# A first layer norm two slots sooner, transposed in 32 by 32 blocks on VectorE and through DRAM

## The chip, the cores and the metric

The kernel runs on one core of a Trainium2 chip. The metric is device time in microseconds of one execution: 1315.79 us as the median of three runs (1315.71 to 1316.1). TensorE does the matrix products, VectorE, ScalarE and GpSimd the elementwise work, SyncE (SP) issues nearly all DMAs. Each of these works through its own instructions in the order in which the kernel writes them.

## The reference

One decoder layer in float32 over `x` of 16 batches, 512 tokens, 256 features. Cut to what matters (B=16, T=512, D=256, 16 heads of 16 dimensions, hidden width 1024):

```python
q = query @ wq + query @ Aq @ Bq * 4;  k = query @ wk;  v = query @ wv + query @ Av @ Bv * 4
q, k = rope(split(q)), rope(split(k))
scores = where(causal, -1e9, einsum('bhqd,bhkd->bhqk', q, k) / 4)
x = layernorm(x + merge(softmax(scores) @ split(v)) @ wo)          # the first norm
h = gelu(butterfly(x @ W_exp + b_exp, up_weights) + up_bias)       # the expansion
y = butterfly(h, down_weights) @ W_con + b_con + down_bias         # the contraction
out = layernorm(x + y)                                             # the second norm
```

## The kernel before

The butterflies are folded into the weights during the first batches, so the feed-forward part of a batch is two dense products: `wup` (256 x 1024) for the expansion and `wdn` (1024 x 256) for the contraction. A batch's residual lies in `zs[b]`, with 128 tokens on the partitions, four token tiles of 256 features.

Everything is laid out on a time table of slots, written by hand. A batch has 20 slots (`per`), so batch b starts at slot s = 20 b, and slot s+41 of batch b is also slot s+21 of batch b+1, s+1 of batch b+2 and s+61 of batch b-1. Four batches are in flight. In every slot the loop at the end of `decoder_layer` issues in this order: score matmuls of two kinds, interleaved in pairs (`weights`, transposed scores that are to be exponentiated, and, 15 slots ahead of them, `largest`, scores whose maxima are wanted); then for each of them what reads it (ScalarE's exponential and GpSimd's causal mask for `weights`, VectorE's masked reductions at L426 for `largest`); then `weigh`, the products of finished exponentials with v; then the functions entered in `others[slot]`, in the order in which they were entered (a lower batch first); then those of `holes[slot]`. The score matmuls of a slot write two PSUM tiles, `pb` and `pa`, each with a single buffer: the next slot's matmuls can only start on them when the readers are through. In most slots `pb` is read by the exponential and `pa` by the reductions; in the last of each five slots both are read by both. All other matmuls take one of three PSUM banks (`bank`).

The feed-forward of batch b follows its attention in these steps, by slot:

- s+40, s+41: `project_out` (the product with wo, L589) and `add_attention` (L601: VectorE adds it to `zs[b]` and takes statistics, one tile at a time); the last tile's `add_attention` in s+42.
- s+42: `spread` (L616: VectorE adds epsilon, GpSimd raises to the power -0.5). s+43, first in the slot: `offset` (L628, VectorE). s+44: `centre` (L635: four ScalarE activations that normalize `zs[b]`).
- s+45: `turn_x1` (L647): eight TensorE transposes of 128 x 128, two VectorE copies into `x1T`, and a GpSimd addition of the bias to `zs[b]` (s+46 for batch 14).
- s+46 to s+49: `hidden` (L664), the expansion in eight chunks of 128 units, two a slot; VectorE copies chunks 0 and 4 out of PSUM, ScalarE the others. s+50: `gelus`. For batch 14 the chunks come in s+47 and later, for batch 15 all at the end.
- s+51 to s+58: `contract` (L691) for tiles 0 to 2, half of the hidden units at a time, and tile 3 in s+63 and s+64, then the second norm (`spread` s+65, `offset` s+67, `centre` and `store` s+68).

In the same slots lie the following of other batches: `project_v` of batch b+2 (its v projections, at s+39 for tile 1, s+42 for tile 2, s+52 for tile 3); the rotary products of batch b+2's q and k on GpSimd (`turn`); `place_largest` of batch b+1 in s+41 (L440: a VectorE transpose of maxima, a DMA to DRAM and two DMAs that put them as a row into q); and `gather` and `invert` of batch b+1 in s+45 and s+46 (a chain of small DMAs for the softmax sums). The softmax of batch b+1 goes on without pause.

Of the kernel before, what the change touches and what calls it, by code (L numbers as in the profile page):

```python
# [11 lines left out]
F32 = mybir.dt.float32  # L12
BF16 = mybir.dt.bfloat16
AF = mybir.ActivationFunctionType
ALU = mybir.AluOpType
PSUM = bass.MemoryType.PSUM

P = 128
NH = 16
DH = 16  # L20
HG = 32
NG = P // HG
# [11 lines left out]
def decoder_layer(  # L34
# [18 lines left out]
    nc = tc.nc  # L53
    B, T, D = x.shape
    NT = T // P
    NC = D // P
    DHID = wcon.shape[0]
    NHC = DHID // P
# [5 lines left out]
    ring2 = ctx.enter_context(tc.tile_pool(name="ring2", bufs=2))  # L64
# [3 lines left out]
    dram = ctx.enter_context(tc.tile_pool(name="dram", bufs=4, space=bass.MemoryType.DRAM))  # L68
# [5 lines left out]
    def bank(name, shape):  # L74
        return ps_w.tile(shape, F32, tag="w", name=name)

    def columns(out, w, moving, start, stop):

        for g in range(NG):
            part = slice(HG * g, HG * (g + 1))  # L80
            nc.tensor.matmul(out[part, :], w[:, part], moving, start=start, stop=stop)  # L81
# [10 lines left out]
    xTs, zs = {}, {}  # L92
# [23 lines left out]
    wdn = const.tile([P, NHC, D], F32, name="wdn")  # L116
    bias2 = const.tile([P, 2, D], F32, name="bias2")
# [337 lines left out]
    state = {}  # L455
# [151 lines left out]
    def stats_of(which, b, t):  # L607
        if t == 0:
            state["stats", which, b] = small.tile(
                [P, NT, 2], F32, tag=f"stats{which}", name=f"stats{which}_{b}"  # L610
            )
        bn = small.tile([P, nc.vector.BN_STATS_DIM], F32, tag="bn", name=f"bn{which}_{b}_{t}")
        nc.vector.bn_stats(bn, zs[b][:, t, :])
        nc.vector.bn_aggr(state["stats", which, b][:, t, :], bn)
# [13 lines left out]
    def offset(which, b, t0=0, t1=NT):  # L628
        stats, norm = state["stats", which, b], state["norm", which, b]
        ts = slice(t0, t1)  # L630
        nc.vector.scalar_tensor_tensor(  # L631
            norm[:, 2, ts], stats[:, ts, 0], -1.0, norm[:, 1, ts], ALU.mult, ALU.mult
        )
# [10 lines left out]
            )  # L644


    def turn_x1(b, c):  # L647
        if c == 0:
            state["x1T", b] = ring2.tile([P, NC, T], F32, tag="x1T", name=f"x1T_{b}", bufs=1)
        pt = bank(f"pt1_{b}_{c}", [P, NT, P])  # L650
        for t in range(NT):
            nc.tensor.transpose(pt[:, t, :], zs[b][:, t, c * P : (c + 1) * P], ident)  # L652
        nc.vector.tensor_copy(
            state["x1T", b][:, c, :], pt.rearrange("p t q -> p (t q)")
        )
        if c == NC - 1:
            nc.gpsimd.tensor_tensor(
                zs[b],
                zs[b],
                bias2[:, 0:1, :].to_broadcast([P, NT, D]),  # L660
                ALU.add,
            )
# [21 lines left out]
    def gelus(b, count=NHC):  # L684
        h = state["h", b]
        for hc in range(count):
            nc.scalar.activation(  # L687
                h[:, hc, :], h[:, hc, :], AF.Gelu, bias=hbias[:, hc : hc + 1]
            )

    def contract(b, t, half):  # L691
        if half == 0:
            state["py"] = bank(f"py_{b}_{t}", [P, D])
        py = state["py"]
        for hc in range(half * NHC // 2, (half + 1) * NHC // 2):
            columns(
                py,
                state["h", b][:, hc, t * P : (t + 1) * P],
                wdn[:, hc, :],
                hc == 0,  # L700
                hc == NHC - 1,
            )
        if half == 1:
            nc.vector.tensor_add(zs[b][:, t, :], py, zs[b][:, t, :])  # L704
            stats_of(2, b, t)

    def store(b):
        nc.sync.dma_start(out[b].rearrange("(t p) d -> p t d", p=P), zs[b])
# [14 lines left out]
    end = B * per + behind  # L723
    last = end + 8
    head = 2
    others = {s: [] for s in range(-head, last)}
    holes = {}
    chains = [(c, side) for c in range(NC) for side in range(2)]

    def add(s, f, *args):  # L730
        others[s].append(lambda: f(*args))

    def start_projection(b, side, c):
        state["pr", b, side, c] = project(b, side, c)
# [13 lines left out]
    for b in range(B):  # L748
        s = b * per
        if b > 0:  # L750

            at = {1: (-16, -11, -13, -9), B - 1: (-3, 2, 10, 10)}.get(b, (-3, -1, 2, 12))
            for t in range(NT):
                add(s + at[t], project_v, b, t)
        if b + 1 < B:

            add(s - head * (b == 0), load_xT, b + 1)
            at = {0: (2, 5, 7, 10), 1: (3, 6, 8, 11)}.get(b, (10, 10, 10, 10))
            for i, (c, side) in enumerate(chains):
                holes.setdefault(s + at[i], []).append(  # L760
                    lambda b=b, side=side, c=c: start_projection(b + 1, side, c)
                )
                turning = s + max(at[0] + 1 + 3 * i, at[i] + 1)
                for step in range(3):
                    add(turning + step, turn, b + 1, side, c, step)
                for step in range(1 + side):
                    add(turning + (6 if i == 3 else 4) + step, part, b + 1, side, c, step)
        add(s + 9, load_x, b)
        add(s + 11, place_largest, b, 0)
        add(s + 21, place_largest, b, 1)  # L770
        for c in range(NC if b + 1 < B else 1):
            if c + 1 < NC:
                add(s + 25 + (b + 1 == B), gather, b, c)
            add(s + (26, 36)[c] + (b + 1 == B), invert, b, c)
            for t in range(NT):
                add(s + ((29, 29, 30, 30), (39, 39, 40, 40))[c][t], scale, b, c, t)
        if b + 1 < B:
            for t in range(NT):
                add(s + (40, 40, 41, 41)[t], project_out, b, t)
                add(s + (40, 40, 41, 42)[t], add_attention, b, t)  # L780
            add(s + 42, spread, 1, b)
            others[s + 43].insert(0, lambda b=b: offset(1, b))
            add(s + 44, centre, 1, b)
            for c in range(NC):
                add(s + 45 + (b + 2 == B), turn_x1, b, c)
        if b + 2 < B:

            late = 2 * (b + 3 == B)
            for hc in range(NHC - late):
                add(s + 46 + hc // 2, hidden, b, hc)  # L790
            holes.setdefault(s + 50, []).insert(0, lambda b=b, late=late: gelus(b, NHC - late))
            for hc in range(NHC - late, NHC):
                holes[s + 50].append(lambda b=b, hc=hc: hidden(b, hc, True))
            for t in range(NT):
                for half in range(2):
                    at = (11, 13, 14, 15, 16, 18, 23, 24)[2 * t + half]
                    if b + 3 == B and t == NT - 1:
                        at = (23, 25)[half]
                    add(s + 40 + at, contract, b, t, half)
            add(s + 65, spread, 2, b)  # L800
            add(s + 67, offset, 2, b)
            add(s + 68, centre, 2, b)
            add(s + 68, store, b)
# [3 lines left out]
    y, z = B - 2, B - 1  # L807
# [4 lines left out]
    for hc, at in ((3, 10), (4, 10), (5, 10), (6, 11), (7, 11)):  # L812
        add(edge + at, hidden, y, hc, True)

    add(end - 3, contract, y, 0, 0)
    add(end - 1, contract, y, 0, 1)
    add(end + 2, contract, y, 1, 0)
    add(end + 2, contract, y, 1, 1)
    for t in range(NT):
        add(end + 2, normalize, z, NC - 1, t)  # L820
    add(end + 2, contract, y, 2, 0)
    for t in range(NT + 1):
        if t < NT:
            add(end + 3, project_out, z, t)
# [2 lines left out]
        if t > 0:  # L827
            add(end + 3, offset, 1, z, t - 1, t)
            add(end + 3, centre, 1, z, t - 1, t)
    add(end + 3, contract, y, 2, 1)  # L830
    add(end + 3, contract, y, 3, 0)
    for c in range(NC):
        add(end + 5, turn_x1, z, c)
    add(end + 5, contract, y, 3, 1)
    for hc in range(NHC):
        add(end + 5, hidden, z, hc, True)
    add(end + 5, spread, 2, y)
# [2 lines left out]
    add(end + 6, store, y)  # L840
    for t in range(NT):
        for half in range(2):
            add(end + 7, contract, z, t, half)
        add(end + 7, finish_tile, z, t)


    first, second = fold_tasks()
# [180 lines left out]
```

## Time and profile before

| what | value |
|---|---|
| median of 3 runs | 1315.79 us |
| profiled execution | 1318.97 us, its span 1317.0 us |
| VectorE, ScalarE, GpSimd busy | 59%, 53%, 43% of the span |
| DMA, mean share of 16 engines | about 18%, 74 MB |
| transposes `pt` (L652) | 128 of 280 ns |
| copies `x1T` (L653) | 32 of 678 ns |
| centre (L638) | 128 of 589 ns |
| mean granted TensorE clock | 0.989 |

The profile is of one execution. A matmul in float32 is listed twice, since the array makes two passes; a transpose is listed once. In a timeline, a line gives start and length in us, engine, source line, operation, output <- inputs, shape and count, and in brackets how long the engine was idle before it and what ended that. The matmuls of a group overlap, so the distance between the starts of two groups is the time that a group cost TensorE. In the table of stretches each engine's busy time stands in the order PE, PEld, DVE, ACT, POOL, then the granted clock, the DMA share and GB/s.

### The profile page before, as it was taken

The numbers are of one execution on the slowest core, as the hardware profiler recorded it, in microseconds if no ns is written. First come the engines' busy times: TensorE is split into PE (matmuls) and PEld (weight loads), VectorE is DVE, ScalarE is ACT, GpSimd is POOL, SyncE is SP. The second block draws the span as 40 slices with busy tenths as digits, with TensorE's granted clock in tenths as the row PEclk, the third lists the DMA queues.
The fourth block names the chain that finished last, engine by engine and source line by source line (L and its number), as shares of the span: only waits on it lengthen the run. The fifth ranks groups of instructions, "written<-read, shape, count | busy, mean of one in ns | idle before, by whom it ended". The sixth has DMA issues, their size and how long they took to land.

```text
span 1317.0 us, 38318 instructions
## 1 busy us (share of the span) xinstructions
PE 1280.6 (97%) x15896; PEld 575.2 (44%) x15896; DVE 780.5 (59%) x2760; ACT 702.9 (53%) x1047; POOL 565.1 (43%) x905
## 2 busy tenths in 40 slices
PE   8888999999999999999999999999999999999998
PEld 3343435444353544435354443535444353444443
DVE  5776746657465665747566574756657474665431
ACT  2574455555646555564655546465555646455643
POOL 4525325445362544536254453625445362532430
PEclk9889999999999999999999999999999999999999
DMA  5411111111212111121211112121211212111101
GB/s 169 132 32 59 40 49 46 56 56 41 82 41 65 47 56 56 41 83 41 69 42 57 56 41 83 41 67 45 56 56 40 83 41 70 41 40 32 43 20 34
DMA packets 64062, 74.07 MB, mean 56 GB/s; under 512 B 23120, under 2 KB 42576, under 8 KB 63888
## 3 DMA queue, kind: packets, MB, share of 16 engines
q1 hardware_dynamic: 60000, 66.07, 16.0%
q10 hardware_dynamic: 3888, 5.55, 1.4%
q8 instruction: 125, 2.05, 0.7%
q14 instruction: 49, 0.40, 0.1%
HBM read 40.17 MB, written 18.06 MB: 44 GB/s over the span
## 4 chain that ended last, share of the span: by engine, by line
PE 92%; DVE 3%; ACT 2%; DMA 1%; issue 1%; POOL 0%; SPq 0%; POOLq 0%; DVEq 0%; ACTq 0%
PE pb L474 21%; PE py L81 17%; PE ph L81 16%; PE po L516 12%; PE pqk L81 8%; PE pa L417 4%; PE pwo L81 4%; PE pvv L81 4%; DVE junk L426 1%; PE pd L81 1%; PE pt L652 1%; PE pa L474 1%; PE pb L417 1%; ACT pT L488 1%; ACT h L687 0%
## 5 line engine op out<-in xcount | busy, mean ns | idle before, releaser
L426 DVE CUSTOM_DVE_ANT_0 junk<-pa,causal 128x384 bf16<-128x384 f32 (+2 forms) x878 | 438.6, 500 | 339.0 <-PE pa L417 271.6
L488 ACT ACTIVATE pT<-pb 128x1024 f32<-128x1024 f32 (+1 forms) x314 | 294.2, 937 | 354.8 <-PE pa L417 183.8
L492 POOL TENSOR_SCALAR_AFFINE_SELECT pT<-pT 128x256 f32<-128x256 f32 x512 | 202.3, 407 | 651.4 <-ACT pT L488 650.4
L474 PE MATMUL pb<-qz,kz 17*128 17x512 f32 (+2 forms) x1756 | 330.9, 475 | 17.6 <-ACT pT L488 11.7
L417 PE MATMUL pa<-kz,qz 32*128 32x384 f32 (+3 forms) x1756 | 330.6, 476 | 3.4 <-DVE mx L426 3.4
L81 PE MATMUL py<-wdn,h 128*32 128x256 f32 x4096 | 244.3, 381 | 0.0
L81 PE MATMUL ph<-x1T,yb 128*32 128x512 f32 x2048 | 231.6, 594 | 0.2 <-ACT h L678 0.2
L474 PEld LDWEIGHTS pb<-qz,kz 17*128 17x128 f32 (+1 forms) x1756 | 142.4, 184 | 196.4 <-issue 92.3
L516 PE MATMUL po<-pT,vaug 128*32 128x512 f32 (+3 forms) x2048 | 180.9, 447 | 1.8 <-POOL pT L492 1.8
L81 PEld LDWEIGHTS py<-wdn,h 128*32 128x32 f32 x4096 | 125.3, 110 | 99.2 <-issue 12.7
L417 PEld LDWEIGHTS pa<-kz,qz 32*128 32x128 f32 (+1 forms) x1756 | 143.2, 185 | 14.6 <-DVE mx L426 11.6
L81 PEld LDWEIGHTS ph<-x1T,yb 128*32 128x32 f32 x2048 | 63.2, 110 | 139.8 <-issue 107.6
L81 PE MATMUL pqk<-xT,wqk 128*32 128x512 f32 x1024 | 117.6, 608 | 0.0
L682 ACT COPY h<-ph 128x512 f32<-128x512 f32 x84 | 49.2, 585 | 117.3 <-PE ph L81 117.2
L516 PEld LDWEIGHTS po<-pT,vaug 128*32 128x32 f32 x2048 | 47.9, 109 | 105.3 <-issue 59.1
L426 DVE DVE_READ_ACCUMULATOR2_ANT mx<- 128x1 f32 x1024 | 84.6, 83 | 0.0
L638 ACT ACTIVATE z<-z,norm 128x256 f32<-128x256 f32 x128 | 66.7, 589 | 23.2 <-DVE norm L631 23.2
L365 POOL TENSOR_TENSOR swap<-swap,rope_sb 128x512 f32<-128x512 f32 x62 | 78.8, 1270 | 0.0
L426 DVE CUSTOM_DVE_ANT_0 junk<-pb,causal 128x256 bf16<-128x256 f32 (+3 forms) x146 | 63.6, 436 | 16.4 <-PE pb L417 2.5
L687 ACT ACTIVATE h<-h,hbias 128x512 f32<-128x512 f32 x113 | 70.8, 709 | 0.2
L704 DVE TENSOR_TENSOR z<-py,z 128x256 f32<-128x256 f32 x64 | 27.2, 425 | 72.9 <-PE py L81 70.6
L81 PE MATMUL pvv<-wv_sb,xT 128*32 128x256 f32 x1024 | 66.5, 379 | 0.0
(91 smaller groups left out, 1192.1 us busy)
## 6 DMA issues: line engine op xcount, KB each, us to landing
xT<-in_xT SPq DMA_DIRECT2D x16, 512.0 KB
swap<-qz SPq DMA_DIRECT2D x64, 128.0 KB
swap<-kz SPq DMA_DIRECT2D x64, 128.0 KB
z<-in_x SPq DMA_DIRECT2D x16, 512.0 KB
wide<-recips SPq DMA_DIRECT2D x31, 256.0 KB
spread<-wide SPq DMA_DIRECT2D x31, 256.0 KB
out_y<-z SPq DMA_DIRECT2D x15, 512.0 KB
x<-x SPq DMA_DIRECT2D x32, 128.0 KB
```

Source lines behind the costliest of these rows:

```text
L81: nc.tensor.matmul(out[part, :], w[:, part], moving, start=start, stop=stop)
L365: engine.tensor_tensor(swap, swap, rope_sb[:, 1, :], ALU.mult)
L417: lambda i=i, rows=rows, at=at, n=n, t=t, ps=ps: nc.tensor.matmul(ps[:, i, at : at + n], q[rows, par, t * P : n], k_[rows, par, 0:n], star ...
L426: lambda i=i, at=at, n=n, t=t, g=g, ps=ps: nc.vector.tensor_tensor_reduce(out=junk[:, 0:n], in0=ps[:, i, at : at + n], in1=causal[:, T - n ...
L474: lambda i=i, rows=rows, at=at, n=n, k=block, ps=ps: nc.tensor.matmul(ps[:, i, at : at + n], kt[rows, par, k * P : (k + 1) * P], qt[rows, ...
L488: nc.scalar.activation(pT[:, heads, 0:n], ps[:, :, at : at + n], AF.Exp)
L492: nc.gpsimd.affine_select(out=diag, in_=diag, pattern=[[0, 2], [1, P]], compare_op=ALU.is_ge, fill=0.0, base=0, channel_multiplier=-1,)
L516: nc.tensor.matmul(po[HG * g : HG * (g + 1), k * P : T], vaugs[b % 2][:, k, NG * c + g, first : first + HG], pT[:, g, at : at + n], start= ...
L638: nc.scalar.activation(zs[b][:, t, :], zs[b][:, t, :], AF.Identity, bias=norm[:, 2, t : t + 1], scale=norm[:, 1, t : t + 1],)
L682: nc.scalar.copy(h, ph)
L687: nc.scalar.activation(h[:, hc, :], h[:, hc, :], AF.Gelu, bias=hbias[:, hc : hc + 1])
L704: nc.vector.tensor_add(zs[b][:, t, :], py, zs[b][:, t, :])
```

## The change

The first norm's last `add_attention` and `spread` move to s+41, `offset` and `centre` to s+42. `turn_x1` is replaced, in batches 0 to 14, by two functions. `turn_blocks` in s+43 transposes each 32 x 32 block of `zs[b]` with one VectorE instruction of 128 x 1024 into `turned`, writes it to DRAM with four DMAs, one for each group of 32 partitions, and makes the GpSimd addition. `fetch_turned`, at the end of s+44, reads the whole (512 KB) into `x1T` with one DMA. Since the tokens come out in the order (group, tile, place in the group), `contract` takes 32 columns of `h` for each of its four column groups, wherever they lie; its matmuls are as many and as large as before. The last batch keeps `turn_x1` and the old order.

The neighbours move with it: the expansion has one chunk in s+46, three in s+47 and two in each of s+48 and s+49; `project_v` of batch b+2, tile 2, goes from s+42 to s+46; the contraction of tile 3 of batch b-1 is cut into four quarters in slots s+42 to s+45 of batch b (before: two halves in s+43, s+44), and the second norm's `spread` comes one slot later. Batch 13 keeps its halves for tile 3.

```diff
+    def turn_blocks(b):
+        state["x1T", b] = ring2.tile([P, NC, T], F32, tag="x1T", name=f"x1T_{b}", bufs=1)
+        turned = ring2.tile([P, D // HG, NT, HG], F32, tag="turned", name=f"turned_{b}", bufs=1)
+        nc.vector.transpose(turned, zs[b].rearrange("p t (k j) -> p k t j", j=HG))
+        rows = dram.tile([D, NG, P], F32, tag="x1rows", name=f"x1rows_{b}")
+        state["x1rows", b] = rows
+        for g in range(NG):
+            nc.sync.dma_start(
+                rows.rearrange("(k j) g q -> j k g q", j=HG)[:, :, g, :],
+                turned[HG * g : HG * (g + 1)].rearrange("j k t i -> j k (t i)"),
+            )
+        nc.gpsimd.tensor_tensor(
+            zs[b],
+            zs[b],
+            bias2[:, 0:1, :].to_broadcast([P, NT, D]),
+            ALU.add,
+        )
+    def fetch_turned(b):
+        rows = state.pop(("x1rows", b))
+        nc.sync.dma_start(state["x1T", b], rows.rearrange("(c p) g q -> p c (g q)", p=P))
...
-    def contract(b, t, half):
+    def contract(b, t, first, past):
...
+            of = h.rearrange("p c (g t i) -> p c t g i", g=NG, i=HG)
+        for hc in range(first, past):
+            for g in range(NG):
+                nc.tensor.matmul(
+                    py[HG * g : HG * (g + 1), :],
+                    of[:, hc, t, g, :],
+                    wdn[:, hc, :],
...
-            at = {1: (-16, -11, -13, -9), B - 1: (-3, 2, 10, 10)}.get(b, (-3, -1, 2, 12))
+            at = {1: (-16, -11, -13, -9), B - 1: (-3, 2, 10, 10)}.get(b, (-3, -1, 6, 12))
...
-                add(s + (40, 40, 41, 42)[t], add_attention, b, t)
-            add(s + 42, spread, 1, b)
-            others[s + 43].insert(0, lambda b=b: offset(1, b))
-            add(s + 44, centre, 1, b)
-            for c in range(NC):
-                add(s + 45 + (b + 2 == B), turn_x1, b, c)
+                add(s + (40, 40, 41, 41)[t], add_attention, b, t)
+            add(s + 41, spread, 1, b)
+            others[s + 42].insert(0, lambda b=b: offset(1, b))
+            add(s + 42, centre, 1, b)
+            add(s + 43, turn_blocks, b)
+            holes.setdefault(s + 44, []).append(lambda b=b: fetch_turned(b))
...
-                add(s + 46 + hc // 2, hidden, b, hc)
+                add(s + (46, 47, 47, 47, 48, 48, 49, 49)[hc], hidden, b, hc)
...
+                for n in range(4):
+                    add(s + 62 + n, contract, b, NT - 1, 2 * n, 2 * n + 2)
+            add(s + 65 + (b + 3 < B), spread, 2, b)
```

More of the change, by code (lines that the diff above doesn't have):

```diff
@@ L689, in gelus, with halves @@
             )
-    def contract(b, t, half):
-        if half == 0:
+    def contract(b, t, first, past):
+        if first == 0:
             state["py"] = bank(f"py_{b}_{t}", [P, D])
         py = state["py"]
[L695 to L703, printed above, removed]
+        h = state["h", b]
+        if b + 1 == B:
+            of = h.rearrange("p c (t g i) -> p c t g i", g=NG, i=HG)
+        else:
+            of = h.rearrange("p c (g t i) -> p c t g i", g=NG, i=HG)
[5 more added lines that the diff above has]
+                    wdn[:, hc, :],
+                    start=(hc == 0),
+                    stop=(hc == NHC - 1),
+                )
+        if past == NHC:
             nc.vector.tensor_add(zs[b][:, t, :], py, zs[b][:, t, :])
             stats_of(2, b, t)
+    def halves(b, t, half):
+        contract(b, t, half * NHC // 2, (half + 1) * NHC // 2)
     def store(b):
@@ L793, in decoder_layer @@
                 holes[s + 50].append(lambda b=b, hc=hc: hidden(b, hc, True))
-            for t in range(NT):
+            for t in range(NT - 1):
                 for half in range(2):
[L796 to L800, printed above, removed]
+                    add(s + 40 + (11, 13, 14, 15, 16, 18)[2 * t + half], halves, b, t, half)
+            if b + 3 == B:
+                for half in range(2):
+                    add(s + (63, 65)[half], halves, b, NT - 1, half)
+            else:
+                for n in range(4):
+                    add(s + 62 + n, contract, b, NT - 1, 2 * n, 2 * n + 2)
+            add(s + 65 + (b + 3 < B), spread, 2, b)
             add(s + 67, offset, 2, b)
@@ L813, in decoder_layer @@
         add(edge + at, hidden, y, hc, True)
[L815 to L818, printed above, removed]
+    add(end - 3, halves, y, 0, 0)
+    add(end - 1, halves, y, 0, 1)
+    add(end + 2, halves, y, 1, 0)
+    add(end + 2, halves, y, 1, 1)
     for t in range(NT):
         add(end + 2, normalize, z, NC - 1, t)
-    add(end + 2, contract, y, 2, 0)
+    add(end + 2, halves, y, 2, 0)
     for t in range(NT + 1):
@@ L829, in decoder_layer @@
             add(end + 3, centre, 1, z, t - 1, t)
-    add(end + 3, contract, y, 2, 1)
-    add(end + 3, contract, y, 3, 0)
+    add(end + 3, halves, y, 2, 1)
+    add(end + 3, halves, y, 3, 0)
     for c in range(NC):
         add(end + 5, turn_x1, z, c)
-    add(end + 5, contract, y, 3, 1)
+    add(end + 5, halves, y, 3, 1)
     for hc in range(NHC):
@@ L842, in decoder_layer @@
         for half in range(2):
-            add(end + 7, contract, z, t, half)
+            add(end + 7, halves, z, t, half)
         add(end + 7, finish_tile, z, t)
```

## The prediction

> **What bounds the kernel now.** I read the engine totals and the chain that ended last first. TensorE is busy 97% of the span and carries 92% of the chain, so a microsecond counts only where TensorE gains or loses it.
>
> ```profile
> PE 1280.6 (97%) x15896; PEld 575.2 (44%) x15896; DVE 780.5 (59%) x2760; ACT 702.9 (53%) x1047; POOL 565.1 (43%) x905
> ...
> PE 92%; DVE 3%; ACT 2%; DMA 1%; issue 1%; POOL 0%; SPq 0%; POOLq 0%; DVEq 0%; ACTq 0%
> ```
>
> Second, the stage. In the timeline the first expansion matmul of a batch comes every 76.6 us. I take batch 5 (s = 100), whose slot s+40 starts at 534.60, and split slots s+41 to s+49 by TensorE's starts (stretch, length, then busy time by engine):
>
> ```profile
> 538.07:541.01 2.94, 2.94 (x45) 1.25 (x41) 2.80 (x10) 1.63 (x2) 1.98 (x4) 1.00 0.60 176
> 541.01:543.95 2.94, 2.94 (x45) 1.40 (x41) 2.38 (x11) 1.02 (x1) 1.58 (x3) 1.00 0.09 22
> 543.95:547.07 3.12, 3.12 (x53) 2.07 (x49) 2.89 (x13) 1.43 (x2) 1.84 (x3) 1.00 0.03 5
> 547.07:551.00 3.93, 3.93 (x68) 2.29 (x65) 2.33 (x11) 2.27 (x5) 2.11 (x5) 1.00 0.01 4
> 551.00:553.66 2.66, 2.66 (x28) 1.32 (x24) 2.42 (x8) 2.30 (x4) 0.32 (x1) 1.00 0.00 0
> ```
>
> TensorE has no hole here, but VectorE (fourth figure) fills 2.80 of 2.94 us in s+41 and 2.89 of 3.12 in s+43: there is little slack behind TensorE.
>
> Third, that slack, in VectorE's timeline around the same slots and in two places where TensorE does wait:
>
> ```profile
> 540.67 0.42 DVE L603 TENSOR_TENSOR z<-pwo,z 128x256 f32<-128x256 f32 x1
> ...
> 541.69 0.18 DVE L444 STREAM_TRANSPOSE mT<-mx 128x32 f32<-128x32 f32 x1
> 542.25 0.56 DVE L426 CUSTOM_DVE_ANT_0 junk<-pa,causal 128x384 bf16<-128x384 f32 x1 [0.38 <-PE pa L417]
> ...
> 543.78 0.29 DVE L426 CUSTOM_DVE_ANT_0 junk<-pa,causal 128x128 bf16<-128x128 f32 x1
> ...
> 547.07 0.60 DVE L631 SCALAR_TENSOR_TENSOR norm<-stats,norm 128x4 f32<-128x4 f32 x1
> ```
>
> ```profile
> 162.14 0.70 PE L474 MATMUL pb<-qz,kz 32*128 32x256 f32 x4 [0.52 <-ACT pT L488]
> 163.05 0.48 PE L417 MATMUL pa<-kz,qz 16*128 16x256 f32 x2 [0.21 <-DVE mx L426]
> ...
> 1197.01 0.59 PE L474 MATMUL pb<-qz,kz 32*128 32x384 f32 x2 [1.41 <-ACT pT L488]
> ```
>
> Scores live in single PSUM tiles, so a slot's score matmuls wait until the exponentials (pb) and the reductions (pa) of the slot before are through. In batch 0's thin slot s+43 that already shows; at 1197 us six gelus (3.78 us) stood ahead of an exponential on ScalarE and TensorE lost 1.41 us.
>
> **The change, part by part.**
>
> *Removed from TensorE.* Eight transposes start at 552.64 and the next score matmul at 553.66: 1.02 us, with about 0.1 us lost before them (0.57 us from the weighing to them, 0.46 where other work follows). Two VectorE copies (1.27 us) go too; they ran beside TensorE and are worth nothing by themselves. All else on TensorE is moved: a half contraction (1.87 us) becomes two quarters of 0.94, one v projection (0.98) goes from s+42 to s+46, one expansion chunk (1.79) from s+46 to s+47. The work of s+41 to s+49 by rows without waits: nine score blocks at 1.07 = 9.63, output projection 1.87, weighing 4.0, quarters 3.74, v 0.98, expansion 14.28: 34.5 us against 35.95 now. The full prize is 1.45 us a batch.
>
> *Norm sooner: VectorE.* add_attention of tile 3 (add, statistics, aggregate: 1.02 us, as tile 2's from 540.67 to 541.69) and the first step of spread (about 0.2) now run in s+41, ahead of place_largest's transpose and of s+42's reductions. VectorE had only 0.38 us of idle there. The reductions start at 543.1 instead of 542.25 and the last ends at 543.1 + 1.82 = 544.92; s+43's pa matmuls, wanted at 543.85, start 0.07 later (as at 163.05), 545.0. The row vector of place_largest leaves 1.2 us later (543.1); what follows it took until about 546 from 541.9, so it arrives near 548, before its use in s+45.
>
> *GpSimd.* The power (1.02) now stands ahead of the rotary product (1.27): it waits for VectorE until 542.9 and ends at 543.95; the product and s+42's masks end at 546, used in s+44. No cost.
>
> *Offset and centre in s+42: ScalarE.* offset starts when the reductions end, 544.93. It took 0.20 us at 561.35 with GpSimd idle, 0.60 at 547.07, where it ended together with a GpSimd product; I take the middle, an end at 545.3. [...]
>
> From 545.3, centre's four activations (2.06) then run 545.35 to 547.4, and behind them on ScalarE's queue stands s+43's exponential, ready at 546.1. It ends at 548.4, and TensorE, done with s+43 at 547.0, starts s+44 at 548.45 (0.06 after, as at 162.14): 1.45 us lost, besides the 1.05 in s+43.
>
> *On to the expansion.* s+44 (1.07 + 0.89 + 0.94) gives 551.35; s+44's reductions end about 551.6, so s+45 starts 551.7; s+45 (1.07 + 0.46 + 0.94) ends 554.15 and s+46's scores 555.3. There the first chunk wants x1T.
>
> *The new way to x1T.* s+43's reductions now run 546.15 to 548.0 (they need all pa matmuls, 1.1 us from 545.0, then 1.85). The block transpose of 128x1024 follows. The 128x32 one takes 193 ns, 39 above the 154 of a 128x1 operation, so 32 times 39 plus 154 gives 1.4; the 128x1024 product of the prologue took 1.18 to 1.23. I take 1.2; below it nothing is near, above it stands 32 x 0.193 = 6.2, if each block paid its start. End 549.2. Four DMA issues of 128 KB: swap's, of the same size, take 0.56 us each, rows' 0.33; I take 0.58 with its gap: the last starts at 551.0. Data of a 128 KB transfer moved within 1.17 + 0.5 us of its issue, and dependent issues came 0.4 to 0.5 us after the last packet: fetch_turned at 553.05. The xT load has the same shape (512 KB, 2 KB rows): 3.5 us from issue to last packet three times out of three, plus the same 0.4: 556.9. Short issues and no receipt give 555.8; a transpose like GpSimd's 128x1024 addition (2.38) and issues of 0.62 give 558.3. Nothing is queued behind fetch_turned on SP before s+45's sums, which TensorE's own delay puts after it. GpSimd's bias addition (2.38) now stands before s+44's masks: done 551.6, masks 552.4, wanted at 552.8.
>
> [...]
>
> *Sum.* Expansion starts at 556.9 instead of 554.78 (+2.1), and the v projection now lies behind it (+0.98): +3.1 us a batch for the twelve batches 1 to 12. Batch 13 keeps its v projection in s+42: +2.1. In batch 0 the stage has long waits already (from s+40 to the expansion 22.47 us against 20.18): 22.3 + 0.98 - 22.47 = +0.8. Batch 14 expands a slot later and pays only the ScalarE wait against its transposes: +0.5. Together 37.2 + 2.1 + 0.8 + 0.5 = 40.6. The profiled execution is 1318.97 us (span 1317.0 and 1.97 around), 0.24% over the median of 1315.79; differences carry over unchanged: 1315.8 + 40.6, about **1356 us**. Its own range is 1342 to 1374 (x1T at 555.8 to 558.3, thirteen batches).
>
> **Rivals.**
> - *The round trip is hidden*: x1T is there by 555.3. Then only the waits of s+43 and s+44 remain, +1.5 us a batch, about 1336. For it: short DMA issues (0.33). Against: the 3.5 us of every 512 KB load.
> - *The norm comes early enough, and it is faster.* One mechanism: VectorE's queue in s+41. If centre ended 2.5 us sooner (544.9), ScalarE would be clear when the exponential is ready and x1T would come near 554.4; break-even is an expansion start of 553.8, centre ending 3.1 us sooner. Further forward, the prize of 1.45 us over thirteen batches gives 1297. For it: VectorE is idle 0.38, 0.72 and 0.80 us between 541 and 551. Against: the adds wait for the projection matmuls, and the idle before the norm is the 0.38 alone.
> - *The transpose or the 512 B rows run slow.* The transpose at 2.4 us and more or writes at half speed: x1T after 559, +5.2 us a batch, about 1385.
> - *Nothing measurable*: losses cancel the prize, 1316.
>
> **How the numbers follow.** Forecast 0.60, round trip hidden 0.10, faster 0.18, slow transpose 0.09, nothing 0.03. This kernel's measurement can tell about 0.2% (2.6 us) from no change. Slower is 0.60 + 0.10 + 0.09 = 0.79. The range of 1306 to 1380 leaves out most of the faster case and more than half of the slow one, about 0.2.
>
> **What would show it.** In the changed profile: the transposes gone from TensorE; VectorE's s+42 reductions 0.85 us late against TensorE; ScalarE's centre directly ahead of s+43's exponential; TensorE waiting about 1.4 us at s+44 "<-ACT pT"; and about 1.6 us before the expansion, for the DMA into x1T. If the expansion starts without waiting on a DMA, the second step is wrong; if s+44 starts within 0.3 us of s+43's end, the first. A batch period of 79.7 us instead of 76.6 confirms the sum.

## The result, and the profile after

The changed kernel takes 1366.95 us (median of six runs, 1363.85 to 1369.46) against 1315.94 us beside it: 1.0384 times as long, 95% interval 1.0362 to 1.0406. The forecast was 1356 us in a range of 1306 to 1380. Its profiled execution took 1363.85 us, its span 1362.1.

The page's engine totals and, below, the shares of the chain that ended last:

```profile
PE 1282.5 (94%) x15776; PEld 562.5 (41%) x15776; DVE 779.2 (57%) x2745; ACT 704.5 (52%) x1047; POOL 566.6 (42%) x905
...
PE 79%; DVE 8%; DMA 7%; ACT 2%; issue 2%; SPq 1%; POOL 0%; DVEq 0%; POOLq 0%; ACTq 0%
```

TensorE has 120 instructions fewer (eight transposes in each of 15 batches) and yet is busy 1.9 us longer. Outside its busy time lie 79.6 us (1362.1 - 1282.5) where there were 36.4. Its share of the chain falls from 92% to 79%, and what enters is VectorE and DMA. The table of TensorE's waits, in total, times and longest, names them:

```profile
PE pb L474 <- ACT pT L488: 33.5, 32, 1.5
PE ph L81 <- DMA x1T<-x1rows: 18.7, 13, 2.3
```

The first stood at 11.7 us before (16 times), the second is new. With the rise of "pb L474 <- issue" from 2.8 to 5.3, these three rows rise by 21.8 + 18.7 + 2.5 = 43.0 us; the idle time as a whole rises by 43.2.

The same batch as before, batch 5, whose slot s+40 now starts at 547.67 us. First the stretches (columns as before), cut at TensorE's starts of slots s+41 to s+47:

```profile
551.15:554.09 2.94, 2.94 (x45) 1.25 (x41) 2.80 (x10) 1.64 (x2) 1.73 (x3) 1.00 0.65 177
554.09:557.02 2.93, 2.93 (x44) 1.40 (x40) 2.72 (x11) 1.02 (x1) 0.90 (x1) 1.00 0.02 7
557.02:561.48 4.46, 3.03 (x36) 1.41 (x32) 3.60 (x16) 2.99 (x5) 3.34 (x5) 1.00 0.06 11
561.48:564.72 3.24, 3.01 (x48) 1.65 (x49) 2.34 (x9) 1.20 (x2) 3.22 (x4) 1.00 0.51 105
564.72:567.37 2.65, 2.65 (x33) 1.14 (x33) 1.29 (x3) 1.42 (x2) 0.95 (x3) 1.00 0.35 77
567.37:572.33 4.96, 4.01 (x45) 1.40 (x41) 3.31 (x11) 1.80 (x3) 1.50 (x3) 1.00 0.39 136
```

The third stretch (s+43) is 4.46 us long with 3.03 of TensorE in it, the last (s+46) 4.96 with 4.01: two clear holes, where there was none. Then the timelines of TensorE, ScalarE, VectorE, GpSimd and SP, each cut to the lines that carry the change:

```profile
554.09 0.59 PE L474 MATMUL pb<-qz,kz 32*128 32x384 f32 x2
554.10 0.59 PE L417 MATMUL pa<-kz,qz 16*128 16x384 f32 x2
...
557.02 0.91 PE L474 MATMUL pb<-qz,kz 32*128 32x384 f32 x4
557.92 0.59 PE L417 MATMUL pa<-kz,qz 16*128 16x384 f32 x2
561.48 0.48 PE L474 MATMUL pb<-qz,kz 32*128 32x256 f32 x2 [1.43 <-ACT pT L488]
569.61 1.93 PE L81 MATMUL ph<-x1T,yb 128*32 128x512 f32 x16 [0.95 <-DMA x1T<-x1rows]
...
558.44 2.08 ACT L638 ACTIVATE z<-z,norm 128x256 f32<-128x256 f32 x4 [2.09 <-DVE norm L631]
560.43 1.00 ACT L488 ACTIVATE pT<-pb 128x1024 f32<-128x1024 f32 x1
...
556.08 0.51 DVE L426 CUSTOM_DVE_ANT_0 junk<-pa,causal 128x384 bf16<-128x384 f32 x1
557.78 0.63 DVE L631 SCALAR_TENSOR_TENSOR norm<-stats,norm 128x4 f32<-128x4 f32 x1
560.85 1.24 DVE L651 STREAM_TRANSPOSE turned<-z 128x1024 f32<-128x1024 f32 x1
...
557.12 1.28 POOL L365 TENSOR_TENSOR swap<-swap,rope_sb 128x512 f32<-128x512 f32 x1
...
562.12 1.85 SPq L655 DMA_DIRECT2D x1rows<-turned  x4
566.14 0.38 SPq L668 DMA_DIRECT2D x1T<-x1rows  x1
```

Read it backwards from the first hole. TensorE's score matmuls of s+44 (561.48) wait for the exponential that ends at 561.43. That one stands on ScalarE directly behind centre's four activations (558.44 to 560.43). Centre waits for offset (VectorE, 557.78 for 0.63 us), and offset for the reductions of s+42, which start at 556.08 because one more `add_attention` (that of tile 3) and the first step of `spread` stand ahead of them. The second hole is the round trip: block transpose 560.85, writes issued from 562.12, fetch at 566.14, first matmul at 569.61.

A third loss does not show as idle time. In s+42 `pb` and `pa` start 0.01 us apart (554.09, 554.10); in s+43 `pa` starts 0.90 after `pb` (557.02, 557.92), since VectorE's reductions of s+42, late by then, read it until 557.86. TensorE counts as busy meanwhile, with the matmuls into `pb`. This is part of why its busy time did not fall with the transposes.

One thing was not in the forecast at all. This stretch begins in s+44 of batch 4, at the end of a wait of 1.42 us; the figure ahead of the DMA share is the granted clock:

```profile
480.55:487.00 6.45, 6.45 (x52) 3.12 (x56) 2.35 (x9) 1.20 (x2) 3.86 (x5) 0.50 0.47 101
```

TensorE is busy throughout, at half its clock. In the profile after there are four such stretches between 200 and 1280 us, at 480.3 (6.8 us), 640.7, 889.9 and 971.8 (3.4 us each); in the profile before there is none. 17 us at half clock are at most 8.5 us lost: less where a later wait would have taken the time anyway.

### The profile page after: what moved, and what is told of

The parts are those of the page before. It is cut to its first block, busy times and chain, and to the rows that moved or that the text cites. A ratio compares the mean times of both kernels' runs of the same rounds, so it can differ in the third digit from the quotient of the medians.

```text
span 1362.1 us, 38182 instructions
## 1 busy us (share of the span) xinstructions
PE 1282.5 (94%) x15776; PEld 562.5 (41%) x15776; DVE 779.2 (57%) x2745; ACT 704.5 (52%) x1047; POOL 566.6 (42%) x905
## 4 chain that ended last, share of the span: by engine, by line
PE 79%; DVE 8%; DMA 7%; ACT 2%; issue 2%; SPq 1%; POOL 0%; DVEq 0%; POOLq 0%; ACTq 0%
PE pb L474 17%; PE ph L81 16%; PE py L725 14%; PE po L516 9%; PE pqk L81 8%; PE pa L417 4%; DVE junk L426 4%; DMA x1T<-x1rows 4%; PE pvv L81 4%; PE pwo L81 3%; DMA x1rows<-turned 3%; SPq L655 1%; PE pb L417 1%; DVE turned L651 1%; ACT pT L488 1%
## 5 line engine op out<-in xcount | busy, mean ns | idle before, releaser
L474 PE MATMUL pb<-qz,kz 17*128 17x512 f32 (+2 forms) x1756 | 333.8, 476 | 41.0 <-ACT pT L488 33.5
L81 PE MATMUL ph<-x1T,yb 128*32 128x512 f32 x2048 | 236.6, 604 | 19.0 <-DMA x1T<-x1rows 18.7
L725 PE MATMUL py<-wdn,h 128*32 128x256 f32 x4096 | 250.0, 382 | 0.0
L474 PEld LDWEIGHTS pb<-qz,kz 17*128 17x128 f32 (+1 forms) x1756 | 141.8, 184 | 219.2 <-issue 78.2
L81 PE MATMUL pwo<-wo_sb,x 128*32 128x256 f32 x1024 | 62.1, 381 | 1.4 <-DVE z L603 0.7
```

The lines of the kernel that those rows point to most:

```text
L474: lambda i=i, rows=rows, at=at, n=n, k=block, ps=ps: nc.tensor.matmul(ps[:, i, at : at + n], kt[rows, par, k * P : (k + 1) * P], qt[rows, ...
L725: nc.tensor.matmul(py[HG * g : HG * (g + 1), :], of[:, hc, t, g, :], wdn[:, hc, :], start=(hc == 0), stop=(hc == NHC - 1),)
```

## The experiments

The theory after the result was the prediction's walk: TensorE pays one wait at s+44, since centre stands ahead of the exponential, and another for x1T. The rivals were a cost of the moved neighbours, a transpose on TensorE that was worth less than its 1.02 us, and the clock.

**Without the wait for x1T.** The expansion of batches 0 to 14 reads a buffer `still` that is filled once at the start. The new norm, transpose and DMAs stay.

```diff
+    still = const.tile([P, NC, T], F32, name="still")
...
+            nc.scalar.dma_start(still, xT[0].rearrange("(c p) t -> p c t", p=P))
...
-                state["x1T", b][:, c, :],
+                (state["x1T", b] if b + 1 == B else still)[:, c, :],
```

> The changed kernel, but the expansion of batches 0 to 14 reads a buffer filled once at the start (the transposes of x of batch 0) instead of x1T. The block transpose, the four writes and the fetch still run; only nobody waits for them, and the expansion of these batches does not see its own input. Theory (three waits, of which the one for x1T is 13 times about 1.4 us, 18.7 us in the profile of the changed kernel, and a part of the half-clock windows that follow the waits): about 1342 us, 1336 to 1348; the wait of s+44 for the exponential stays at 1.4 us. Rival (the new order of the neighbours and the narrow columns of the contraction cost the time, the waits only show it elsewhere): 1358 or more.

Measured 1339.72 us, 1.0188 [1.0160, 1.0215]. So waiting for x1T costs 27 us (1366.95 - 1339.72): the 18.7 us of the waits' table, and up to 5.1 for the half clock, of which one stretch of 6.8 us is left between 200 and 1280 us (10.2 us less). The remaining 3 us are not accounted for. The wait at s+44 is untouched, in the timeline of TensorE:

```profile
556.05 0.48 PE L476 MATMUL pb<-qz,kz 32*128 32x256 f32 x2 [1.42 <-ACT pT L490]
```

**Centre a slot later.** It then stands behind the exponential of s+43 instead of ahead of it; the round trip starts later. A second kernel does this and reads `still` as well.

```diff
-            add(s + 42, centre, 1, b)
+            add(s + 43, centre, 1, b)
             add(s + 43, turn_blocks, b)
```

> The changed kernel with centre one slot later, in s+43 ahead of turn_blocks, so that the exponential of s+43 comes first on ScalarE. Theory (the two waits lie on the same chain through centre; x1T arrives about 1.2 us later than now): the wait at s+44 goes from 1.4 us to about 0.3 or less, the wait for x1T grows from about 1.4 to about 4, and the time is about 1380 us, 1370 to 1390. Rival (each wait has its own price, and the one at s+44 is given back): about 1346 us, 14 times 1.4 less.

> Both edits at once: centre in s+43, and the expansion of batches 0 to 14 reads the buffer filled at the start (it does not see its own input). Theory: what stays is the wait of about 1 us for VectorE's reductions in s+43 and a short one behind centre, together about as much as the eight transposes were worth: about 1317 us, 1308 to 1326. Rival of the neighbours' order: 1335 or more.

Measured 1382.46 us, 1.0513 [1.0486, 1.0539], and with `still` 1341.06, 1.0196 [1.0171, 1.0222]. The first is as expected, the second a plain miss: taking centre out of the exponential's way was to save some 22 us against the kernel above (1339.72 to 1317) and saved nothing. TensorE's timelines say where it went, of centre later:

```profile
568.07 0.70 PE L474 MATMUL pb<-qz,kz 17*128 17x512 f32 x2 [1.13 <-ACT pT L488]
573.59 2.79 PE L81 MATMUL ph<-x1T,yb 128*32 128x512 f32 x12 [1.61 <-DMA x1T<-x1rows]
```

and of the same with `still`:

```profile
558.53 0.48 PE L419 MATMUL pa<-kz,qz 16*128 16x256 f32 x2 [0.30 <-DVE mx L428]
562.65 0.70 PE L476 MATMUL pb<-qz,kz 17*128 17x512 f32 x2 [1.12 <-ACT pT L490]
```

The wait of 1.43 us has become one of 1.12 a slot later, and the reductions of s+43 now hold `pa` up at s+44. The profile after already had a sign of that: s+43's reductions end at 560.93 there, only 0.5 us before the exponential, so that without centre in the way `pa` would still have held TensorE for some 0.9 us (an estimate: from 560.05, the end of its work, to 560.93). The wait of 1.12 us is listed against an exponential, but VectorE's timeline of the kernel with centre later shows what held TensorE there:

```profile
564.88 1.25 DVE L651 STREAM_TRANSPOSE turned<-z 128x1024 f32<-128x1024 f32 x1 [0.99 <-ACT z L638]
566.05 0.39 DVE L426 CUSTOM_DVE_ANT_0 junk<-pa,causal 128x256 bf16<-128x256 f32 x1
...
567.53 0.42 DVE L426 CUSTOM_DVE_ANT_0 junk<-pb,causal 128x256 bf16<-128x256 f32 x1
```

The block transpose waits for centre, and s+44's reductions stand behind it on VectorE. They end at 567.96; the last exponential, which reads `pa` behind the first two of them, ends at 567.56; s+45's scores start at 568.07. So neither of the two places tried for centre spares TensorE a wait: in one ScalarE's queue passes it on, in the other VectorE's. Expansion starts 22.97 us after s+40's start instead of 21.94, the waits for x1T add up to 28.1 us in 14 places (18.7 us in 13), and the profile has nine half-clock stretches (mean clock 0.982 against the change's 0.986); the size of the first expectation was right, its split was not.

**The neighbours alone.** The kernel before, with only the v projection, the expansion's chunks, the quarters and the second norm's `spread` where the change puts them.

```diff
-(-3, -1, 2, 12)
+(-3, -1, 6, 12)
-                add(s + 46 + hc // 2, hidden, b, hc)
+                add(s + (46, 47, 47, 47, 48, 48, 49, 49)[hc], hidden, b, hc)
+                    elif t == NT - 1:
+                        for q in (2 * half, 2 * half + 1):
+                            add(s + 62 + q, contract, b, t, half, q)
+                        continue
-            add(s + 65, spread, 2, b)
+            add(s + 65 + (b + 3 < B), spread, 2, b)
```

> The kernel before with only the neighbours moved as in the change: project_v of tile 2 in s+46, the expansion 1, 3, 2, 2 over s+46 to s+49, tile 3 of the contraction in quarters in s+62 to s+65, the second spread a slot later. Norm, transposes on TensorE and the order of the tokens as before. Theory: the work is the same and TensorE has it in the same stretch, so within 4 us of before, 1312 to 1320. Rival (the order of the neighbours costs): 1335 or more.

Measured 1335.82 us, 1.0141 [1.0109, 1.0172]: the rival, not the theory. The norm is at its old place here, and still a batch takes 77.83 us instead of 76.60. (The profiled execution, 1328.78 us, is the fastest of four; the others took 1335.03 to 1336.65.) TensorE's and VectorE's timelines of this kernel, around s+43 and s+44 of batch 5:

```profile
545.03 0.70 PE L474 MATMUL pb<-qz,kz 32*128 32x256 f32 x4
546.03 0.48 PE L417 MATMUL pa<-kz,qz 16*128 16x256 f32 x2 [0.30 <-DVE mx L426]
...
543.95 0.17 DVE L625 TENSOR_SCALAR norm<-stats 128x4 f32<-128x4 f32 x1
544.14 0.56 DVE L426 CUSTOM_DVE_ANT_0 junk<-pa,causal 128x384 bf16<-128x384 f32 x1
545.67 0.29 DVE L426 CUSTOM_DVE_ANT_0 junk<-pa,causal 128x128 bf16<-128x128 f32 x1
```

In the kernel before, `pb` and `pa` of s+44 start 0.14 us apart (547.07 and 547.21). Here `pa` starts a microsecond after `pb`, because VectorE's reductions of s+43 begin at 544.14, behind the norm, and end at 545.97. Before, the half contraction in s+43 (1.87 us) covered that; a quarter (0.94) does not. Most of the 1.23 us a batch is seen here. Twelve batches of 1.23 make 15 of the 19 us; the rest was not traced.

**The transposes left out.** The kernel before, without the eight transposes and their copies; the expansion reads `still`. And the same with the first chunk of the expansion put into s+45, the slot that the transposes left.

```diff
     def turn_x1(b, c):
+        if b + 1 < B:
+            if c == NC - 1:
+                nc.gpsimd.tensor_tensor(zs[b], zs[b], bias2[:, 0:1, :].to_broadcast([P, NT, D]), ALU.add)
+            return
```

```diff
-                add(s + 46 + hc // 2, hidden, b, hc)
+                add(s + (46 + hc // 2 if hc else 45), hidden, b, hc)
```

> The kernel before without the eight transposes and the two copies of batches 0 to 14, the expansion of these batches reads the buffer filled at the start (it does not see its own input); all slots as before. Theory after the first four runs (a slot can't be shorter than its score matmuls, the reductions or exponential behind them and VectorE's other work; s+45 with 2.66 us stands at that floor, its transposes only fill it): nothing or little, 1310 to 1317 us. Rival (the prediction's step: 1.1 us of TensorE a batch are worth 1.1 us): 1299, 1296 to 1303.

> The same, with the first chunk of the expansion in s+45 instead of s+46, so that s+45 holds 3.3 us and s+46 2.9 us of matmuls, both above the floor of 2.65. Theory: now the 1.1 us come out, 14 times: about 1300 us, 1296 to 1305. Rival (the floor has nothing to do with it): the same time as without the move.

Measured 1315.22 us, 0.9990 [0.9973, 1.0008], and refilled 1301.10, 0.9883 [0.9861, 0.9906]. Taking 1.02 us a batch off the bounding engine is worth nothing that these runs can tell. TensorE's timeline without the transposes, s+45 and s+46:

```profile
550.00 0.70 PE L476 MATMUL pb<-qz,kz 17*128 17x512 f32 x2
...
552.31 0.70 PE L476 MATMUL pb<-qz,kz 17*128 17x512 f32 x2 [0.60 <-ACT pT L490]
552.72 0.70 PE L419 MATMUL pa<-kz,qz 32*128 32x512 f32 x2
...
553.77 3.64 PE L81 MATMUL ph<-still,yb 128*32 128x512 f32 x32
```

From s+45's start to the expansion it takes 3.77 us; with the transposes it took 3.78 (551.00 to 554.78). A slot has a floor: its score matmuls, the exponential and the reductions that read them, and only then the next scores into the same two PSUM tiles. s+45 stood on that floor, and 0.60 us of wait and 0.41 of `pa` behind `pb` took the transposes' place. With a chunk of the expansion in the slot both are gone:

```profile
543.22 0.70 PE L476 MATMUL pb<-qz,kz 17*128 17x512 f32 x2
...
544.74 1.90 PE L81 MATMUL ph<-still,yb 128*32 128x512 f32 x16
546.58 0.70 PE L476 MATMUL pb<-qz,kz 17*128 17x512 f32 x2
546.59 0.70 PE L419 MATMUL pa<-kz,qz 32*128 32x512 f32 x2
```

So about 15 us is what the transposes are worth where the expansion's input costs nothing and is there a slot sooner. That is a bound, as this kernel does not compute the expansion's input. The change puts the expansion's work later, not sooner.

**The changed kernel with its neighbours at their old places**: v projection in s+42, two chunks a slot from s+46, halves in s+43 and s+44, `spread` at s+65.

```diff
-(-3, -1, 6, 12)
+(-3, -1, 2, 12)
-                add(s + (46, 47, 47, 47, 48, 48, 49, 49)[hc], hidden, b, hc)
+                add(s + 46 + hc // 2, hidden, b, hc)
-                for n in range(4):
-                    add(s + 62 + n, contract, b, NT - 1, 2 * n, 2 * n + 2)
+                for half in range(2):
+                    add(s + (63, 64)[half], halves, b, NT - 1, half)
-            add(s + 65 + (b + 3 < B), spread, 2, b)
+            add(s + 65, spread, 2, b)
```

> The changed kernel with the neighbours where they were: project_v of tile 2 in s+42, the expansion two chunks a slot, tile 3 of the contraction in halves in s+63 and s+64, the second spread in s+65. Norm, block transpose and round trip as changed. Theory (thicker slots s+43 and s+44 cover a part of what VectorE and ScalarE do there, and the v projection no longer lies behind the expansion): the wait behind centre falls to about 0.5 us, the wait for x1T stays, about 1347 us, 1340 to 1354. Rival (the new neighbours are what makes the early norm bearable): 1366 or more.

Measured 1357.86 us, 1.0312 [1.0291, 1.0333], outside the expected 1340 to 1354. The direction is the theory's, the gain 9 us and not 20. TensorE's timeline of this kernel:

```profile
559.14 0.48 PE L474 MATMUL pb<-qz,kz 32*128 32x256 f32 x2 [0.83 <-ACT pT L488]
565.26 0.70 PE L474 MATMUL pb<-qz,kz 17*128 17x512 f32 x2 [0.60 <-ACT pT L488]
567.24 3.21 PE L81 MATMUL ph<-x1T,yb 128*32 128x512 f32 x28 [0.44 <-DMA x1T<-x1rows]
```

The thicker s+43 covers 0.6 us more of centre. (`pa` of s+43 still starts 0.90 us behind `pb`, at 555.31 after 554.41: that loss comes from the earlier norm, with either set of neighbours.) But s+45 now has neither transposes nor a quarter, falls to its floor, and waits the same 0.60 us as the kernel without transposes: that was not expected. Three half-clock stretches remain.

**The clock.** Useless 128 x 128 transposes on TensorE fill the waits of s+43 and s+46: twelve and ten in one kernel, eleven and eight (batches 0 to 13) in another, the latter beside the unchanged kernel of the change, run again.

```diff
+    def fill(b, n, at):
+        pf = bank(f"pf_{b}_{at}", [P, P])
+        for _ in range(n):
+            nc.tensor.transpose(pf, ident, ident)
...
             add(s + 43, turn_blocks, b)
+            if b + 2 < B:
+                add(s + 43, fill, b, 11, 43)
...
+            add(s + 46, fill, b, 8, 46)
             for hc in range(NHC - late):
```

> The changed kernel with useless transposes of the identity where TensorE waits: 12 at the end of s+43 (1.3 us) and 10 ahead of the expansion in s+46 (1.1 us). Theory (after some of the waits the granted clock goes to half for 3.4 or 6.8 us, 8.5 us of time in the profile of the changed kernel; with the waits filled it stays up): the waits stay as long as they are, the clock shows no half window after 200 us, 1359 us, 1353 to 1363. Rival (the half windows have another cause): 1365 to 1372, with half windows as before.

> The changed kernel once more, beside the next run on the same chip: 1366 us, 1362 to 1371, three to six windows at half clock between 200 and 1280 us of the profiled execution.

> The changed kernel with useless transposes in the waits of batches 0 to 13 as before, but a little fewer (11 at the end of s+43, 8 ahead of the expansion), so that they end before the wait does. Theory (the waits also cost clock): no half window, or one, between 200 and 1280 us, and 5 to 8 us less than the changed kernel beside it: about 1359 us. Rival (the half windows cost nothing that the next wait would not have taken anyway): within 2 us of the changed kernel.

Measured: with twelve and ten 1364.24 us, 1.0349 [1.0313, 1.0386], which the spread of its runs (1356.61 to 1367.01) leaves undecided; the change again 1364.89, 1.0375 [1.0350, 1.0400]; with eleven and eight 1358.14, 1.0335 [1.0307, 1.0362], 6.75 us less. The stretch 200 to 1280 us of the change, run again, and of the kernel filled with eleven and eight:

```profile
200.00:1280.00 1080.00, 1031.44 (x12972) 456.26 (x12964) 630.03 (x2259) 567.88 (x802) 466.64 (x741) 0.99 0.21 64
...
200.00:1280.00 1080.00, 1059.37 (x13244) 482.34 (x13240) 629.61 (x2258) 570.47 (x806) 471.86 (x750) 1.00 0.21 64
```

The mean clock is 0.99 against 1.00: two half-clock stretches of 6.8 us (at 809 and 1045; three to six were expected) against none. With twelve and ten there is none in that stretch either. From the first expansion matmul of batch 1 to that of batch 13, the filled kernels need 957.9 us each, the unfilled one 962.4 in both of its profiles. In TensorE's timelines these matmuls are, first of the change run again and then of the kernel with eleven and eight:

```profile
251.79 1.92 PE L81 MATMUL ph<-x1T,yb 128*32 128x512 f32 x16 [1.27 <-DMA x1T<-x1rows]
1214.22 1.92 PE L81 MATMUL ph<-x1T,yb 128*32 128x512 f32 x16 [1.62 <-DMA x1T<-x1rows]
...
247.30 1.92 PE L81 MATMUL ph<-x1T,yb 128*32 128x512 f32 x16 [0.58 <-DMA x1T<-x1rows]
1205.17 1.92 PE L81 MATMUL ph<-x1T,yb 128*32 128x512 f32 x16 [0.74 <-DMA x1T<-x1rows]
```

So more work on TensorE makes the kernel no slower, and where the waits are filled the clock stays up and some 4.5 us of these batches are saved; that is shown. That the filling saves the whole 6.75 us is not: the rest lies outside these batches. Over the first 200 us the granted clock was 0.96 with eleven and eight and 0.93 in the kernel beside it, and most of that difference lies ahead of the first filled wait; with twelve and ten the kernel as a whole shows no clear gain.

No kernel that computes the whole layer was faster than the one before.

## Why the prediction was right, and where it was wrong

The sign, the place of the waits and nearly all of the walk were right; 40.6 us were summed and 51.0 measured (44.9 between the two profiled executions).

- **The walk from s+40 to the expansion** holds within 0.4 us. Relative to s+40's start: `pa` of s+43 at +10.40, measured +10.25 (557.92 - 547.67); s+44 at +13.85, measured +13.81, with a wait of 1.43 for 1.45 (and in s+43 0.90 for 1.05 for `pa`); s+45 +17.10 and +17.05; the fetch +18.45 and +18.47; the expansion +22.30 and +21.94, after a wait of 0.95 us for 1.6. This batch takes 79.2 us, where 79.7 was forecast; it is the quickest of the twelve, and the waits for x1T average 1.44 us (18.7 in 13). The first rival (round trip hidden) falls with these waits, the third (slow transpose) with the next point. The walk put the s+44 wait down to centre. Centre does end it, but the reductions of s+43 alone would have made some 0.9 of its 1.43 us, so moving centre could not give it back.
- **The transpose** took 1.24 us, 1.2 taken from two rows; 6.2 had been the bound. The four issues were quicker than taken (0.46 us each for 0.58), and the block of 512 KB came back 3.42 us after its issue against 3.5, with TensorE following 0.04 after it against 0.4. That the fetch fits to 0.02 us is luck: the last write was issued 0.6 us sooner than walked (+15.83 for +16.40), and the fetch then came 2.64 us after it for 2.05. In the chain of the changed kernel the writes and the load stand so:

```profile
563.50 2.51 DMA x1rows<-turned
566.14 3.42 DMA x1T<-x1rows
```

- **Offset** took 0.63 us and ended at 558.41, with GpSimd's product, which ran from 557.12 to 558.40. The sum took a middle (0.37 us, end at 545.3). In the profile after, the 13 offsets beside such a product (batches 1 to 13) took 0.61 to 0.63 us, and each ended within 0.03 us of it; in the profile before, the one at 1239.52, beside GpSimd's bias addition (1239.46 to 1241.83), took 2.33. Nor was GpSimd idle at 561.35, as the prediction has it: a mask ran there until about 561.5, when the offset of 0.20 us ended too. The difference of 0.26 us was made up elsewhere in the walk, as the reductions ended a little sooner.
- **"The full prize is 1.45 us a batch"** was the wrong step of the sum's logic. A TensorE without holes was read as one that gains whatever is taken off it. The transposes left out alone gave 1315.22 against 1316.45: nothing, since s+45 falls to its floor. The prize needs other work in that very slot (1301.10), and the rival "faster, 1297" rested on it. The forecast itself was walked slot by slot along VectorE and ScalarE, so this step entered its 40.6 us only in batch 14's 0.5, which sets the wait against the transposes' price.
- **"All else on TensorE is moved"** costed the quarters and the moved v projection, in the prize, at nothing but their place. The neighbours alone cost 19 us (1335.82 against 1316.53): a thinned s+43 no longer covers VectorE's reductions, and s+44's `pa` waits even with the norm at its old place. The walk had the thin slots in it, but put its waits down to the earlier norm alone.
- **Missing from the sum: the granted clock.** The waits were costed at their own length. From the first expansion matmul of batch 1 to that of batch 13 the profile before takes 921.0 us (247.67 to 1168.69) and the profile after 962.4 (250.25 to 1212.69): 41.4 more for the twelve batches, where the sum had 37.2. The filled kernels, without a half-clock stretch there, take 36.9 more (957.9). So the waits by themselves come to about what was summed, and about 4.5 us behind them are half clock. Outside the twelve batches the profiles differ by 3.5 us and the sum had 3.4; that match is not a test of these terms, since over the first 200 us the granted clock was 0.93 before and 0.95 after. The medians differ by 51.0 and the two profiles by 44.9 because the profiled execution of the changed kernel is its fastest of six, 3.1 us below their median, and that of the kernel before lies 3.0 above its own. The other five executions of the changed kernel had a mean clock of 0.976 to 0.985 against its 0.986, so part of the 6 us between is clock too; how much was not traced.
- **Hidden work that was costed at nothing** stayed so: GpSimd's bias addition ran from 562.24 to 564.62, and none of the larger waits of TensorE in this stage is for GpSimd.

By kernels, the loss is: neighbours +19, norm and block transpose without the wait for x1T +4 more (1339.72), the wait for x1T with its half-clock stretches +27. These steps do not add in another order: in the changed kernel the neighbours make 9 us. What the wait behind centre costs by itself stays open, since no run removed it without another wait taking its place.

## What to carry to other kernels

Where each slot reuses single PSUM buffers, as here, look for a floor under a slot, set by their readers: s+45 stood at 2.66 us, and 1.02 us of transposes taken out of it gave nothing (1315.22 us against 1316.45). Take work off the bounding engine only in slots above the floor, or put other work there in the same edit (1301.10). Before thinning a slot, list what its work covers on the other engines, and cost those waits even for edits that only move work (19 us here). When one engine's wait is removed, look at which other engine would have held the same buffer almost as long (1.43 us behind ScalarE became 1.12 a slot later, behind VectorE). Count half-clock stretches beside the waits: here four of them, of 3.4 and 6.8 us, began within 0.3 us of the ends of waits, and useless matmuls in unavoidable waits saved some 4.5 us over twelve batches.

## What the runs showed of the hardware that was not expected

- Half-clock stretches began right at the ends of waits as short as 1.41 us. In the changed kernel's profile three last 3.41 us and one twice that; all four begin within 0.3 us of a wait's end: behind 1.42 us at 480.55, 1.41 at 640.68, 1.63 at 889.81 and 2.22 at 971.95. Not every such wait has a stretch behind it: there are 13 for x1T and 16 more than before for exponentials, and four stretches; the longest, 2.29 us at 809.46, has none. What decides it stays open.
- Writing 512 KB in rows of 512 B and reading it back in rows of 2 KB cost 8.8 us from the start of the block transpose to the first matmul (560.85 to 569.61), of which the transpose is 1.24 us.
- One VectorE instruction transposes all 128 blocks of 32 x 32 in 1.24 us, little more than the 1.18 to 1.23 us of a plain product of that size.
